# List products in float16, three one-hot matrices kept in SBUF, and an earlier gate for one layer's weights, in a sparse graph network on one core

## The chip, the cores and the metric

The kernel runs on one NeuronCore of a Trainium2 chip. The metric is the device time of one execution in microseconds, measured over several runs. One further execution was taken with the hardware profiler; its instructions, waits and DMA transfers are what the views below show. The engines are named as in the profile: PE (TensorE, with PEld for its weight loads), DVE (VectorE), ACT (ScalarE), POOL (GpSimd) and SP (SyncE, which here only issues DMAs). PSUM is the memory that PE writes its results to, SBUF the working memory, and DRAM stands for the memory outside the core.

## The reference

The input is `x`, 8 graphs of 2048 nodes with 128 features each, and one adjacency matrix `adj` (2048 x 2048, symmetric, with the diagonal set) that all layers and all eight graphs share. About 1 in 128 of its entries is set, so a node has some 17 neighbours. Four layers follow each other. Layers 0 and 2 are attention layers, cut to what matters:

```python
Q = (h @ Wq).reshape(B, N, 8, 16); K = ...; V = ...
scores = einsum('bnhd,bmhd->bhnm', Q, K) / sqrt(16)
scores = where(adj == 0, -inf, scores)
attn_out = einsum('bhnm,bmhd->bnhd', softmax(scores), V)
x = layer_norm(h + attn_out @ Wo + bo)
x = layer_norm(x + relu(x @ W1 + b1) @ W2 + b2)
```

Layers 1 and 3 are graph attention layers:

```python
h = x @ W; e = leaky_relu((h @ a_src)[:, :, None] + (h @ a_dst)[:, None, :])
e = where(adj == 0, -inf, e)
x = layer_norm(softmax(e) @ h + x)
```

Since most of the adjacency matrix is zero, only the set entries have to be computed.

## The kernel before, in words

**Gathering.** The kernel doesn't multiply by the full matrix. For each layer it writes a table in DRAM with one row per node, which holds the keys and values of all eight graphs (layers 0 and 2) or the projected features and a score (layers 1 and 3). A *unit* is 64 nodes; there are 32 units, and a *block* is two units (128 rows of `adj`). Each unit has a list of its edges, packed into nine tiles of 128 places, and the tiles are handled in four pairs and one single (`TG` is 5). For each tile POOL issues an indirect DMA (`gather`, L1647) that brings 128 table rows into SBUF: in an attention layer these are 8 KB rows, so a tile is 1 MB. A pair of tiles fills one of six `kv` buffers.

**The lists.** `block_list` and `unit_list` make them from `adj`, during the first part of layer 0 only. One adjacency block is read (L1045), DVE marks the columns (L1053) and finds up to 40 neighbours per row with repeated maximum searches (L1071 to L1096). Then PE multiplies the row degrees with constant 0/1 matrices (`before`, `upto`, `middle`, `same_unit`, `same_group`): this gives the prefix sums that say where each row's edges begin and end in the list (`places`, L1120; into the PSUM tile `ps_off`). ACT copies them beside the neighbours into the tile `aux` (`ends`, L1125). For each of the block's two units PE selects its 64 rows (`ps_aux`, L1175), ACT splits the result (`split`, L1185 to L1196), three ACT steps over 640 elements make a one-hot matrix from places to rows (`targets`, L1205 to L1209), and PE multiplies it with the neighbours (`ps_l`, L1229 to L1240). DVE picks each place's neighbour from that (`sources` and `ones`, L1255 to L1267), and ACT writes the indices for the gathers (L1277 to L1279). All these products are float32, each of which the profile records as two passes. The first four units (`LATE` is 4) have some extra steps, so that their first gathers don't need the last table rows.

**One-hot matrices.** The one-hot matrix of a unit, `hot`, is needed again by the attention layers: it spreads the unit's queries over its edges (`qe`, L1710) and adds the weighted values back per node (`acc` and `sums`, L1780). So ACT narrows it to fp8 (`hot8`, L1283), a DMA stores it to DRAM (`hots`, L1287; on POOL's queue for the first twelve units, on SP's after that), and `fetch` loads it again for each attention layer (L1362) and widens it on ACT (L1369). There are three buffers of `hot` and two of `hot8`; a `hot8` buffer is free again when its store has landed.

**Attention for a pair of tiles.** DVE multiplies the gathered keys with the spread queries (L1722) and sums over each head (L1729), ACT takes the exponential (L1739), POOL or DVE weighs the values (L1748), and PE adds them up (L1780). After the five steps of a unit come the output projection, two normalisations and the feed-forward network. The graph layers are built alike, with smaller rows.

**The setup.** Before the first gather, the table of layer 0 has to be there: the 32 units' features are loaded (L1324), projected on PE (`ps_p`, L1509), copied by ACT or DVE into one of three row buffers (`trows`, L1447 and L1449) and stored by SP (L1566). The first lists are made at the same time.

**What sets the order.** A planner (`Plan`) holds every operation with a key, estimated costs and its dependencies, simulates the engines with these costs, and so fixes the order in which each engine gets its instructions. Lower keys go first; list work of block `i` has keys about `10*i - 60`, attention work of unit `u` has keys about `5*u`, so the lists lead by about twelve units. On the chip, each engine takes its instructions strictly in that order, and waits where an input isn't ready. A buffer is taken when an operation is planned, from a fixed number per kind (`SBUF_BUFS`, `PSUM_BUFS`); `m`, the PSUM kind that lists and projections share, has two.

**Weights.** `fill` issues the small loads of a layer's weights on SP. Each load reads a *gate*, a cell whose writers must be done first. In `run`, the gate of layer 1's weights is `gates[24]`, the projection of unit 24; the later layers' gate is `x_at[8]`, the store of unit 8 of the layer before. `gat_weights` (L985) then needs PE and DVE for a few short steps (L1001 to L1018).

Of the kernel before, what the change touches and what calls it, by code (L numbers as in the profile page):

```python
# [9 lines left out]
F32 = mybir.dt.float32  # L10
# [33 lines left out]
PAIRS = TG - 1  # L44
QB = 4
# [5 lines left out]
    "kv": 6, "hot": 3, "hot8": 2, "x": 4, "q_sb": 2, "rows": 3, "at": 1, "r": 2, "x1": 2, "hidden": 1, "normed": 2,  # L51
    "xnew": 2, "trows": 2, "s": 2, "var": 2, "rstd": 2, "rc": 2, "te": 2, "e": 4, "w": 3,
    "cand": 2, "aux": 3, "unit_aux": 2, "some": 2, "rank_e": 2, "pick": 1,
# [714 lines left out]
class Sparse:  # L768
# [15 lines left out]
    def __init__(self, ctx, tc, x, xt, xk, adj, w, out):  # L784
# [42 lines left out]
        self.hots_at = [Cell() for _ in range(self.NU)]  # L827
        self.ends_at = [None] * self.NU
# [9 lines left out]
        self.shift = self.const.tile([P, LATE, 2], F32, name="shift")  # L838
# [5 lines left out]
        self.junk = self.const.tile([P, P], F32, name="junk")  # L844
# [8 lines left out]
    def constants(self):  # L853
# [49 lines left out]
        for g in range(P // GROUP):  # L903
            nc.gpsimd.memset(self.strip[g * GROUP : (g + 1) * GROUP, g, :], 1.0)
        self.before = const.tile([P, P], F32, name="before")
        nc.gpsimd.affine_select(
            out=self.before,
# [7 lines left out]
        for g in range(1, P // GROUP):  # L915
            nc.gpsimd.memset(self.before[0 : g * GROUP, g * GROUP : (g + 1) * GROUP], 0.0)
        self.upto = const.tile([P, P], F32, name="upto")
        nc.vector.tensor_tensor(self.upto, self.before, self.ident, ALU.add)
        self.same_unit = const.tile([P, P], F32, name="same_unit")
        nc.gpsimd.memset(self.same_unit, 0.0)  # L920
        for p in range(2):
            nc.gpsimd.memset(self.same_unit[p * UNIT : (p + 1) * UNIT, p * UNIT : (p + 1) * UNIT], 1.0)
        self.same_group = const.tile([P, P], F32, name="same_group")
        nc.gpsimd.memset(self.same_group, 0.0)
        for g in range(P // GROUP):
            part = slice(g * GROUP, (g + 1) * GROUP)
            nc.gpsimd.memset(self.same_group[part, part], 1.0)
        self.middle = const.tile([P, P], F32, name="middle")
        nc.vector.tensor_tensor(self.middle, self.before, self.upto, ALU.add)

        nc.vector.tensor_scalar(self.before, self.before, -1.0, None, ALU.mult)

        self.to_unit = []
        for p in range(2):
            t = const.tile([P, 2, UNIT], F32, name=f"to_unit_{p}")
            for hf in range(2):
                nc.vector.tensor_copy(t[:, hf, :], self.ident[:, p * UNIT : (p + 1) * UNIT])
            self.to_unit.append(t.rearrange("p h t -> p (h t)"))
# [99 lines left out]
    def block_list(self, adj, i):  # L1038
# [40 lines left out]
        aux = cell("aux", [P, wide])  # L1079
        some = cell("some", [P, DEG])  # L1080

        def largest(e):
            c = cand.tile.rearrange("p q c -> p (q c)")
            if late:
                e.tensor_scalar(
                    some.tile[:, 0:8], cand.tile[:, 15, :], 0.0, 0.0, ALU.is_gt, ALU.add, accum_out=aux.tile[:, WIDE + 2 : wide]
                )
            for r in range(DEG // 8):
# [5 lines left out]
                some.tile, aux.tile[:, 0:DEG], 0.0, 0.0, ALU.is_gt, ALU.add, accum_out=aux.tile[:, DEG + 4 : WIDE]  # L1094
            )
            e.tensor_reduce(self.seen[:, 1, i : i + 1], aux.tile[:, 0:DEG], axis=mybir.AxisListType.X, op=ALU.add)  # L1096
            if late:
                deg = aux.tile[:, DEG + 4 : WIDE]
                e.tensor_tensor(deg, deg, aux.tile[:, WIDE + 2 : wide], ALU.subtract)

        op({"DVE": 3.5}, largest, key + 0.2, reads=[cand], writes=[aux, some])
        ps = cell("m", [P, CH], name="ps_off")

        def places(e):
            deg = aux.tile[:, DEG + 4 : WIDE]
            after = aux.tile[:, wide - 1 : wide]
            for c, (w, x) in enumerate(
                (
                    (self.before, deg),
                    (self.upto, self.ones[:, 0:1]),  # L1110
                    (self.upto, self.ones[:, 0:1]),
                    (self.middle, deg),
                    *(
                        ((self.same_group, deg), (self.before, after), (self.middle, after), (self.upto, after))
                        if late
                        else ((self.upto, deg), (self.same_unit, deg))
                    ),
                )
            ):
                e.matmul(ps.tile[:, c : c + 1], lhsT=w, rhs=x, start=True, stop=True)  # L1120

        op({"PE": 0.8}, places, key, reads=[aux], writes=[ps])

        def ends(e):
            e.copy(aux.tile[:, DEG : DEG + 4], ps.tile[:, 0:4])  # L1125
            if not late:
                e.copy(self.seen[:, 2:4, i], ps.tile[:, 4:6])

        op({"ACT": 0.45}, ends, key + 0.3, reads=[ps], writes=[aux])
        if late:  # L1130
            self.late_places(i, aux, ps, key)
        for p in range(2):
            self.unit_list(2 * i + p, p, aux, key + 5 * p)

    def late_places(self, i, aux, ps, key):

        op = self.op
        gap = self.cell("gap", [P, 3])

        def places(e):  # L1140
            deg, after = aux.tile[:, DEG + 4 : WIDE], aux.tile[:, WIDE + 2 : WIDE + 3]
            begin, more, both = gap.tile[:, 0:1], gap.tile[:, 1:2], gap.tile[:, 2:3]
            e.tensor_scalar(begin, ps.tile[:, 4:5], float(PAIRS * P), None, ALU.max)
            e.scalar_tensor_tensor(more, ps.tile[:, 5:6], deg, begin, ALU.add, ALU.subtract)
            e.tensor_tensor(aux.tile[:, WIDE : WIDE + 1], more, ps.tile[:, 0:1], ALU.subtract)
            e.scalar_tensor_tensor(aux.tile[:, WIDE + 1 : WIDE + 2], begin, 2.0, ps.tile[:, 6:7], ALU.mult, ALU.add)
            e.tensor_tensor(self.seen[:, 2, i : i + 1], begin, ps.tile[:, 7:8], ALU.add)
            e.scalar_tensor_tensor(both, begin, 1.0 / GROUP, after, ALU.mult, ALU.add)

        op({"DVE": 0.6}, places, key + 0.3, reads=[ps], writes=[aux, gap])  # L1150
        total = self.cell("m", [P, CH], name="ps_total")
        op(
            {"PE": 0.2},
# [10 lines left out]
    def unit_list(self, u, p, block_aux, key):  # L1164
        op, cell = self.op, self.cell
        ps = cell("m", [P, CH], name="ps_aux")
        aux = cell("unit_aux", [P, 2, DEG + 3])
# [32 lines left out]


        def targets(e, f):
            oht = hot.tile[:, 0:GS]
# [11 lines left out]
        if late:  # L1215
            op({"ACT": 0.3}, lambda e: self.late_targets(e, after.tile, u), key + 0.3, reads=[ends], writes=[after])

            def both(e):
                e.tensor_scalar(after.tile, after.tile, self.late_ends[:, u, 1:2], None, ALU.is_le)
                shared = hot.tile[:, GS - P : GS]  # L1220
                e.tensor_tensor(shared, shared, after.tile, ALU.add)
# [5 lines left out]
        def parts(e):  # L1227
            for t in range(TG):
                e.matmul(  # L1229
                    ps_l.tile[:, 2 * t : 2 * t + 2, :].rearrange("p j c -> p (j c)"),  # L1230
                    lhsT=hot.tile[:, t * P : (t + 1) * P],
# [4 lines left out]
            if late:  # L1236
                e.matmul(
                    ps_l.tile[:, 2 * PAIRS : 2 * TG, DEG], lhsT=after.tile, rhs=self.shift[:, u, :], start=False, stop=False
# [3 lines left out]
                lhsT=hot.tile[:, GS - P : GS],  # L1242
# [5 lines left out]
        op({"PE": 1.0}, parts, key, reads=[hot, aux, *([after] if late else [])], writes=[ps_l])  # L1248
# [13 lines left out]
        def ones(e):  # L1262
            self.slots(e, hot, ps_l.tile[:, :, DEG + 1].rearrange("p (t j) -> p t j", j=2))
# [19 lines left out]
        op({"ACT": 1.05}, lambda e: e.activation(hot8.tile, hot.tile, AF.Copy, saturate=False), key, reads=[hot], writes=[hot8])  # L1283
# [10 lines left out]
    def slots(self, e, hot, owner):  # L1294
# [3 lines left out]
            hot.tile[:, GS:HOT].rearrange("p (t j c) -> p t j c", j=2, t=TG),  # L1298
# [906 lines left out]
```

## Time and profile before

| | |
|---|---|
| median of 3 runs | 2985.49 us (2976.74 to 2986.78) |
| the profiled execution | 2981.53 us, span 2979.8 us |
| PE, DVE, POOL, ACT busy | 79%, 77%, 72%, 47% of the span |
| first gather issued | 124.72 us |
| first multiply of attention (L1722) | 163.30 us |
| layer 0 ends, about | 1150 us |

The span runs from the first to the last instruction of the core; the profiled execution is about 1.7 us longer than its span. In the views, a line starts with the source line and the engine, then comes the operation with its output and inputs by name, and then busy time, count or mean. A wait is written as `[us <-who]`: so long was the engine idle, and that instruction or DMA ended the wait. In the table by stage, each row is a stretch of the span with the busy microseconds of each engine in it.

### The profile page before, as it was taken

To read this page: it belongs to the slowest core of one execution; us is meant where nothing else is said; L and a number is where in the kernel's file an instruction comes from. 1 tells how busy PE (TensorE), PEld (TensorE's weight loads), DVE (VectorE), ACT (ScalarE), POOL (GpSimd) and SP (SyncE) were. 2 spreads that over 40 slices of the span, in tenths; PEclk is the share of its full clock that TensorE was granted. 3 is DMA by queue.
4 is the path that set the end of the run, shared out by engine and by line. 5 is a ranking of instruction groups with operands and counts; after the bars stand their busy time and mean duration, and the time that the engine had idled before them with its cause. 6 is when DMAs were issued, how large, how long until landed. Compare 5 with 4: busy or idle time off the path is not lost. (4 is left out here: it accounts for less than half of the span.)

```text
span 2979.8 us, 60236 instructions
## 1 busy us (share of the span) xinstructions
PE 2346.3 (79%) x22064; PEld 1401.5 (47%) x22064; DVE 2302.5 (77%) x3775; ACT 1414.5 (47%) x4821; POOL 2138.6 (72%) x1459
## 2 busy tenths in 40 slices
PE   7877888888878787687777688888888887777775
PEld 6733444444433334576665243334333333566664
DVE  6779998899887777555554888988898898576665
ACT  4535555455544443455554144444444444354443
POOL 1158887788887875666664778878888786677774
PEclk8759999899999888889998789999999999887887
DMA  7749998888898886999998998999998997899996
GB/s 288 304 180 361 353 348 308 337 321 341 338 352 320 321 306 254 358 408 407 396 404 323 352 350 341 376 347 363 365 369 345 358 365 279 324 406 399 400 398 265
DMA packets 248495, 1022.93 MB, mean 343 GB/s; under 512 B 39232, under 2 KB 53312, under 8 KB 176288
## 3 DMA queue, kind: packets, MB, share of 16 engines
q0 software_dynamic: 166464, 864.44, 74.9%
q1 hardware_dynamic: 81728, 154.55, 14.1%
q8 instruction: 177, 2.90, 0.4%
q14 instruction: 126, 1.03, 0.1%
HBM read 978.59 MB, written 88.08 MB: 358 GB/s over the span
## 5 line engine op out<-in xcount | busy, mean ns | idle before, releaser
L1647 POOL DMA_INDIRECT kv<-table,idx x1152 | 1198.0, 1040 | 588.0 <-issue 285.2
L1748 POOL TENSOR_TENSOR kv<-kv 128x2048 f32<-128x2048 f32 (+1 forms) x259 | 926.6, 3589 | 96.9 <-ACT kv L1739 92.7
L1722 DVE TENSOR_TENSOR kv<-qe,kv 128x2048 f32<-128x2048 f32 (+1 forms) x320 | 662.0, 2069 | 115.0 <-DMA kv<-table,idx 69.9
L1729 DVE TENSOR_REDUCE s<-kv 128x128 f32<-128x2048 f32 (+1 forms) x320 | 659.5, 2061 | 9.3
L1710 PE MATMUL qe<-q_sb,hot 32*128 32x512 f32 (+1 forms) x2304 | 398.2, 695 | 156.0 <-DVE kv L1722 152.3
L1780 PE MATMUL acc<-kv,hot 128*32 128x512 f32 (+1 forms) x2304 | 370.0, 656 | 47.0 <-POOL kv L1748 24.7
L1984 PE MATMUL acc_q<-kv,w 128*32 128x129 f32 (+1 forms) x4608 | 202.1, 308 | 121.5 <-DVE w L1968 96.9
L1968 DVE TENSOR_TENSOR w<-hot,e 128x512 f32<-128x512 f32 (+1 forms) x384 | 221.2, 597 | 50.3 <-ACT e L1958 37.0
L1710 PEld LDWEIGHTS qe<-q_sb,hot 32*128 32x128 f32 (+1 forms) x2304 | 106.7, 196 | 289.5 <-DVE kv L1722 235.2
L1739 ACT ACTIVATE kv<-s 128x128 f32<-128x128 f32 (+1 forms) x320 | 95.3, 298 | 300.2 <-DVE s L1729 193.2
L1984 PEld LDWEIGHTS acc_q<-kv,w 128*32 128x32 f32 (+1 forms) x4608 | 158.2, 126 | 151.5 <-DVE w L1968 109.5
L1946 DVE TENSOR_TENSOR e<-te,kv 128x16 f32<-128x16 f32 (+1 forms) x320 | 58.3, 182 | 215.7 <-DMA kv<-table,idx 212.8
L1583 ACT ACTIVATE junk<-ps_c 128x128 f32<-128x128 f32 x494 | 136.5, 276 | 158.6 <-PE ps_c L1471 140.7
L1447 ACT COPY trows<-ps_p 128x258 f32<-128x258 f32 (+1 forms) x240 | 113.8, 476 | 187.9 <-PE ps_p L1511 103.7
L1780 PEld LDWEIGHTS sums<-kv,hot 128*32 128x32 f32 (+1 forms) x2304 | 90.1, 120 | 212.4 <-issue 206.8
L1958 ACT ACTIVATE e<-e 128x16 f32<-128x16 f32 (+1 forms) x320 | 64.9, 212 | 243.6 <-DVE e L1953 238.3
L1471 PE MATMUL ps_c<-centre,r 128*128 128x128 f32 x1024 | 153.3, 296 | 32.3 <-DVE r L1857 15.6
L1481 PE MATMUL ps_f<-x,W 128*128 128x512 f32 (+1 forms) x264 | 155.7, 674 | 23.5 <-ACT hidden L1877 16.2
L1471 PEld LDWEIGHTS ps_c<-centre,r 128*128 128x128 f32 x1024 | 132.3, 202 | 74.1 <-DVE r L1857 33.7
L1984 PE MATMUL acc<-kv,w 128*32 128x129 f32 (+1 forms) x2304 | 116.4, 303 | 50.1 <-DVE w L1968 36.2
L1887 PE MATMUL ps_y<-hidden,W 128*128 128x512 f32 (+1 forms) x264 | 146.7, 644 | 6.2 <-ACT hidden L1877 5.7
L1780 PEld LDWEIGHTS acc<-kv,hot 128*32 128x32 f32 (+1 forms) x2304 | 55.7, 115 | 197.6 <-issue 107.6
(201 smaller groups left out, 4015.2 us busy)
## 6 DMA issues: line engine op xcount, KB each, us to landing
x<-xd SPq DMA_DIRECT2D x96, 256.0 KB
xd<-xnew SPq DMA_DIRECT2D x93, 256.0 KB
kv<-table,idx POOLq DMA_INDIRECT x1152
table<-trows SPq DMA_DIRECT2D x128, 130.0 KB
kv<-adj_dram SPq DMA_DIRECT2D x16, 1024.0 KB
table<-trows SPq DMA_DIRECT2D x32, 512.0 KB
table<-trows SPq DMA_DIRECT2D x64, 256.0 KB
kv<-xk_dram SPq DMA_DIRECT2D x8, 1024.0 KB
```

Of the source, the lines that this page charges most:

```text
L1471: e.matmul(ps.tile[:, cols], lhsT=flat(x.tile)[:, cols], rhs=self.centre, start=True, stop=True)
L1481: lambda e: e.matmul(ps.tile, lhsT=w, rhs=x.tile, start=True, stop=True),
L1583: e.activation(self.junk, x, AF.Square, scale=P**-0.5, accum_out=var.tile[:, b, 1:2])
L1647: e.indirect_dma_start(out=rows(kv.tile, j), out_offset=None, in_=self.tables[n][0:nodes], in_offset=bass.IndirectOffsetOnAxis(ap=self.idx ...
L1710: e.matmul(qe.tile[:, j, hf, :], lhsT=hot.tile[rows, t * P : (t + 1) * P], rhs=q.tile[rows, :], start=True, stop=True,)
L1722: e.tensor_tensor(k, qe.tile[:, 0:tiles].rearrange("p j h c -> p (j h) c"), k, ALU.mult)
L1729: e.tensor_reduce(s.tile[:, 0 : tiles * heads].rearrange("p (q c) -> p q c", q=2 * tiles), k, axis=mybir.AxisListType.X, op=ALU.add,)
L1748: e.tensor_tensor(v, v, w.unsqueeze(3).to_broadcast([P, 2 * tiles, heads // 2, HD]), ALU.mult)
L1780: e.matmul(out[rows, :], lhsT=hot.tile[:, col : col + GROUP * (3 - tiles)], rhs=rhs[:, 2 * j + hf, :], start=(t == 0), stop=(t == TG - 1),)
L1887: lambda e, f=f, ps=ps: e.matmul(ps.tile, lhsT=L["W2"][:, f, :], rhs=hidden.tile[:, f, :], start=(f == 0), stop=(f == FFN // P - 1),),
L1968: e.tensor_tensor(w.tile[:, :, j : j + tiles, :].rearrange("p x j c -> p j x c"), oh[:, j : j + tiles].unsqueeze(2).to_broadcast(shape), e ...
L1984: e.matmul(acc(b)[at : at + GROUP * (3 - tiles), :], lhsT=w.tile[:, hf * hb + b, j : j + 3 - tiles, :].rearrange("p j c -> p (j c)"), rhs= ...
```

## The change

It has three parts.

**Float16 lists.** The constant matrices `before`, `same_unit`, `same_group` and `to_unit`, the tiles `unit_aux`, `gap` and `shift`, and a new tile `aux16` are float16, and the one-hot matrix of a list is written as float16 into half of the same `hot` buffer; `upto` and `middle` are gone. Per block there are two products in `places` (three for the first two blocks) in place of six (eight). The ends of the rows, which were products of their own, are now computed on ACT from the row's begin and its degree; the place of a row in its group is a constant, `number`. A new ACT operation, `narrow`, copies the neighbours and degrees from `aux` to `aux16`. Some constants are set by DVE instead of POOL. All values are small whole numbers, which float16 holds.

**Kept matrices.** `hot8` has five buffers. `unit_list` remembers each unit's `hot8`, and for the first three units of layer 0 `fetch` copies from that tile, with no load; their stores to DRAM remain, since layer 2 reads them.

**Gate.** Layer 1's weights have the gate `x_at[3]` instead of `gates[24]`.

```diff
+KEPT = 3
-    "kv": 6, "hot": 3, "hot8": 2, "x": 4, ...
+    "kv": 6, "hot": 3, "hot8": 5, "x": 4, ...
...
+        aux16 = cell("aux16", [P, wide], F16)
+        def narrow(e):
+            e.copy(aux16.tile[:, 0:DEG], aux.tile[:, 0:DEG])
+            e.copy(aux16.tile[:, DEG + 4 : WIDE], aux.tile[:, DEG : DEG + 1])
+            if late:
+                e.copy(aux16.tile[:, WIDE + 2 : wide], aux.tile[:, DEG + 1 :])
+            e.copy(aux16.tile[:, DEG + 1 : DEG + 3], self.number)
+        op({"ACT": 0.7}, narrow, key + 0.2, reads=[aux], writes=[aux16])
         def places(e):
-            deg = aux.tile[:, DEG + 4 : WIDE]
-            after = aux.tile[:, wide - 1 : wide]
-            for c, (w, x) in enumerate(
-                (
-                    (self.before, deg),
-                    (self.upto, self.ones[:, 0:1]),
-                    (self.upto, self.ones[:, 0:1]),
-                    (self.middle, deg),
-                    *(
-                        ((self.same_group, deg), (self.before, after), (self.middle, after), (self.upto, after))
-                        if late
-                        else ((self.upto, deg), (self.same_unit, deg))
-                    ),
-                )
-            ):
-                e.matmul(ps.tile[:, c : c + 1], lhsT=w, rhs=x, start=True, stop=True)
-        op({"PE": 0.8}, places, key, reads=[aux], writes=[ps])
+            deg = aux16.tile[:, DEG + 4 : WIDE]
+            e.matmul(ps.tile[:, 0:1], lhsT=self.before, rhs=deg, start=True, stop=True)
+            if late:
+                e.matmul(ps.tile[:, 1:2], lhsT=self.same_group, rhs=deg, start=True, stop=True)
+                e.matmul(ps.tile[:, 2:3], lhsT=self.before, rhs=aux16.tile[:, WIDE + 2 : wide], start=True, stop=True)
+            else:
+                e.matmul(ps.tile[:, 1:2], lhsT=self.same_unit, rhs=deg, start=True, stop=True)
+        op({"PE": 0.4}, places, key, reads=[aux16], writes=[ps])
         def ends(e):
-            e.copy(aux.tile[:, DEG : DEG + 4], ps.tile[:, 0:4])
+            e.copy(aux16.tile[:, DEG : DEG + 1], ps.tile[:, 0:1])
+            deg = aux.tile[:, DEG : DEG + 1]
+            e.activation(aux16.tile[:, DEG + 3 : DEG + 4], ps.tile[:, 0:1], AF.Identity, bias=deg, scale=-2.0)
             if not late:
-                e.copy(self.seen[:, 2:4, i], ps.tile[:, 4:6])
+                e.activation(self.seen[:, 2, i : i + 1], ps.tile[:, 0:1], AF.Identity, bias=deg, scale=-1.0)
+                e.copy(self.seen[:, 3, i : i + 1], ps.tile[:, 1:2])
...
-        aux = cell("unit_aux", [P, 2, DEG + 3])
+        aux = cell("unit_aux", [P, 2, DEG + 3], F16)
...
+        def hot16():
+            return hot.tile[:, 0 : HOT // 2].bitcast(F16)
...
-        op({"PE": 1.0}, parts, key, reads=[hot, aux, *([after] if late else [])], writes=[ps_l])
+        op({"PE": 0.8}, parts, key, reads=[hot, aux, *([after] if late else [])], writes=[ps_l])
...
         hot8 = cell("hot8", [P, HOT], F8)
+        self.kept[u] = hot8
...
         hot = self.cell("hot", [P, HOT])
+        if n == 0 and u < KEPT:
+            hot8 = self.kept[u]
+            self.op({"ACT": 1.05}, lambda e: e.copy(hot.tile, hot8.tile), key - 15, reads=[hot8], writes=[hot])
+            return x, hot
         if LAYERS[n] is MHA:
...
         self.gate = self.gates[16]
         self.layers[0] = self.mha_weights(0)
-        self.gate = self.gates[24]
+        self.gate = self.x_at[3]
         for n, kind in enumerate(LAYERS):
```

## The prediction

> **What bounds the kernel now.** I read the page first, then the busy time by stage, then the waits of SP and the timeline of the stage that the change touches. Page, head and part 1:
>
> ```profile
> span 2979.8 us, 60236 instructions
> PE 2346.3 (79%) x22064; PEld 1401.5 (47%) x22064; DVE 2302.5 (77%) x3775; ACT 1414.5 (47%) x4821; POOL 2138.6 (72%) x1459
> ```
>
> No engine is full over the span, so stages decide. Busy time by stage (columns: us, then PE, PEld, DVE, ACT, POOL, then PE clock, DMA share, GB/s); cuts at the first gather, the first multiply of attention, the start of unit 4, the end of the lists and the end of layer 0:
>
> ```profile
> 0.00:124.70 124.70, 97.69 (x432) 79.56 (x432) 88.06 (x328) 64.61 (x165) 10.47 (x42) 0.85 0.76 281
> 124.70:163.30 38.60, 29.93 (x125) 26.35 (x125) 15.73 (x50) 19.75 (x61) 13.43 (x15) 0.51 0.83 330
> 163.30:285.20 121.90, 94.66 (x595) 44.37 (x596) 109.88 (x129) 48.79 (x141) 93.26 (x50) 0.76 0.69 260
> 285.20:700.00 414.80, 342.93 (x2359) 175.54 (x2358) 384.53 (x514) 222.60 (x724) 329.92 (x178) 0.92 0.88 332
> 700.00:1150.00 450.00, 360.91 (x2486) 174.69 (x2484) 370.93 (x291) 205.27 (x692) 356.62 (x194) 0.93 0.85 323
> ```
>
> From 163.3 to 700 DVE is 92% busy (494.4 of 536.7): it carries attention and the rest of the lists, and is the bound. Before 163.3 it is busy 103.8 and idle 59.5. Up to 124.7 PE leads (97.7); from there to 163.3 nobody leads: 38.6 us pass with DVE busy 15.7. Every microsecond of DVE idleness removed before 163.3 moves the DVE-bound stretch, and all behind it, forward. What is waited for there, from SP's waits and the timelines of the engines:
>
> ```profile
> SPq L1362 <- DMA hots<-hot: 45.9, 3, 24.4
> 152.31 8.72 SPq L1362 DMA_DIRECT2D hot<-hots  x2
> 124.72 1.07 POOL L1647 DMA_INDIRECT kv<-table,idx  x1 [7.51 <-PE ps_p L1509]
> 136.36 0.56 POOL L1287 DMA_DIRECT2D hots<-hot  x1 [0.86 <-ACT ends L1186]
> 139.07 0.60 ACT L1805 COPY q_sb<-ps_q 128x512 f32<-128x512 f32 x1
> 160.08 1.01 ACT L1369 CAST hot<-hot 128x960 f32<-128x960 fp8e5 x1
> 161.14 2.09 PE L1710 MATMUL qe<-q_sb,hot 32*128 32x512 f32 x8 [1.66 <-ACT hot L1369]
> 163.30 2.29 DVE L1722 TENSOR_TENSOR kv<-qe,kv 128x2048 f32<-128x2048 f32 x1 [2.17 <-PE qe L1710]
> ```
>
> The queries are in SBUF at 139.7, but SP fetches the first one-hot matrix only at 152.3: it needs one of two `hot8` buffers, and their stores, issued on POOL's queue at 134.9 and 136.4 behind eight 1 MB gathers, land 16 us later. The spread (161.1) and the multiply (163.3) follow. In the PE groups of the setup (7 to 125 us) the list products are these and their like:
>
> ```profile
> L1509 PE MATMUL ps_p<-Wkv,kv 128*128 128x256 f32 x252 | 77.1, 462 | 21.0 <-ACT trows L1447 8.0 <-DMA kv<-xk_dram 7.4 <-ACT seen L1127 2.7
> L1229 PE MATMUL ps_l<-unit_aux,hot 128*128 128x86 f32 x60 | 7.8, 280 | 0.0
> L1120 PE MATMUL ps_off<-ones,upto 128*128 128x1 f32 x24 | 4.0, 269 | 0.0
> ```
>
> All list groups of that view sum to 30.8 us (ps_off 15.8, ps_l with its two corrections 11.2, ps_aux 3.1, ps_total 0.7); each float32 product stands as two passes of about 0.28 us.
>
> [...]
>
> **The change, part by part.**
>
> *Kept matrices.* Units 0 to 2 lose SP's load and its wait; the copy reads the kept fp8 tile. In the changed program's order on ACT, unit 0's copy stands among the last projections, long before the query copy, so the spread then waits for `q_sb` alone. With the setup as it is: last row copy ends at 127.3 (DVE, L1449). Between it and the query copy ACT has 7.4 us: one index set with its fp8 copy (0.30+0.25+0.16+1.01), two `unit_aux`/`ends` sets (0.94 each), the three 640-wide steps (0.82+0.85+0.75), four small copies (0.75), the query copy (0.60). I allow 5 for hand-overs (ACT waited 4.9 and 5.7 there in two places). Then four small ACT steps 0.75, which free a PSUM buffer, ps_aux 0.3, the spread 2.1, hops 1: first multiply at 144. The first pair of gathers, 2 MB at 400 GB/s from 124.7, is in by about 132: not late. So 163.3 becomes 144: -19.3.
>
> *Half-width and fewer products.* Up to the last projection the new order has 12 ps_off, 9 ps_aux, 2 ps_total and 52 ps_l products (eight units, not six). [...] Bounds: nothing, if a 16-bit product costs two passes; 19, if PE alone set the pace. DVE (88 of 124.7) and ACT come next, and two more units' list work (ACT some 11 us) now falls into the setup, so I take half: -9.
>
> *ACT and DVE around it.* Each block gains narrowing copies and a scaled step, about 0.75 us of ACT net; 16 blocks make 12 us on an engine 54% busy while the lists run, covered by DVE's backlog and a list lead of twelve units; the five blocks before the first multiply would cost 3.8 if exposed. Memsets move from POOL to DVE ahead of the first adjacency row, where DVE stood idle: nothing. The other DVE instructions keep their sizes.
>
> *Weights of layer 1.* The new gate is `x_at[3]`, but at that point of `run` no store of unit 3 exists, so the gate is empty. In the order the five loads stand as SP's 9th to 13th DMAs, before the first table store. This frees 3.1 us of SP at 109 to 113, where stores wait for ACT's rows anyway: nothing. At the start each of SP's DMAs waits for an earlier one eight places back, so the first three stores (13.5 to 16.5 before) now wait for the second and third adjacency loads (15.4 and at most 23.5), and ACT for row buffers behind them (it waited 5.7 and 0.9 there): bounds 0 and +6; I take +2. ps_w and the six DVE steps (1.3 us) move early too, same work; their 8.1 us stall at 155 goes with them and is inside the -19.3.
>
> *Sum.* First multiply at 163.3 - 19.3 - 9 + 2 = 137. The new order has done nine units' picks by then, not eleven: 2 x 2.33 = 4.7 us of DVE comes back. By unit 4 both orders hold the same DVE work (15 picks, 10 adjacency passes, 9 searches), so idle time is what counts: 59.5 before, 137 - 99.1 = 37.9 after: -21.6. From 163 to 700 DVE also waits 4.3 for ps_l and 10.3 for the spread; shorter list products ahead of them on PE give about 4. From the end of layer 0 on, the order of every engine is identical, so the shift is carried: -26. On the profiled execution 2981.53 (span 2979.8) that is 2955.5; on the median 2985.49, which lies 4 above it, 2959.
>
> **Rivals.** *Setup shrinks by all of PE's 19* (PE leads with 97.7; against it: DVE then needs 93 of some 105): 10 more, 2949 or below. *Setup doesn't shrink* (late first stores, the extra ACT step, PSUM's two `m` buffers): the round trip alone, -19.3 + 4.7 - 4, and +2 to +6 for the stores: about 2970. *The stall is refilled by another:* the kept matrices hold two of three `hot` buffers while lists are made, or gathers, DMA share 0.88 from 285 on, become the bound. Then the gain shrinks to under 9: 2981. Against it: the share is 0.69 until 285, and four units (38 MB) fit into the 140 us from a gather at 118 to unit 4 at 259. *Slower:* POOL is in order, and the eighth one-hot store now stands after only two gathers, waiting for ACT's fp8 copy, seven gathers behind it, and one more store ahead of the first weighing. Before, such stores held POOL 8.3 and 8.0 us. If the copy waits for the whole list chain, gathers starve; it takes 35 us (26 + 9) of starvation to pass 0.3% on the slow side, so about 2996. Against it: the chain is done within some 10 us of the last projection. That the weights don't load behind unit 4 I hold as certain; it is in the sum.
>
> **How the numbers follow.** 0.3%, 9 us, is about what a measurement of this kernel can tell from no change. Main case 0.56 (own range 2950 to 2967); setup fully shorter 0.12; round trip alone 0.18; refilled 0.08; slower 0.06. The first three are faster by over 9: 0.86. Range: 2939 (setup at its bound plus shorter PE waits all along) to 2977 (round trip alone, with late stores).
>
> **What would show it.** Right: SP no longer waits on `hots` before the first spread; the first multiply stands near 137, its releaser the spread behind `q_sb`; ps_l passes number 5 a unit at under 0.2; unit 4 starts near 260; layers 1 to 3 keep their lengths. Wrong: a first gather later than 124.7, a wait on `trows` or `hots` in the first 40 us that is longer than before, DVE waiting on gathers before unit 4, or a layer that changes length after 1150.

## The result and the profile after

The changed kernel takes 2961.92 us in the median (2960.0 to 2966.09) where the kernel before, timed beside it, takes 2985.65: a ratio of 0.993, interval 0.9911 to 0.995. Its profiled execution took 2960.0 us, with a span of 2958.3. The forecast was 2959 (2955.5 for the profiled execution), so the total was met within 3 us on the median. What lies under it was met only in part. The page's head and first part, changed kernel:

```profile
span 2958.3 us, 59482 instructions
PE 2282.4 (77%) x21668; PEld 1334.4 (45%) x21668; DVE 2305.8 (78%) x3785; ACT 1423.9 (48%) x4899; POOL 2137.4 (72%) x1455
```

PE lost 64 us of work (2346.3 to 2282.4), the other engines none: the gain is in idle time. Busy time by stage, with the columns as before and the cuts at this kernel's own first gather, first multiply and unit 4:

```profile
0.00:129.10 129.10, 84.21 (x337) 61.95 (x337) 97.78 (x371) 74.08 (x209) 10.29 (x39) 0.80 0.75 276
129.10:139.95 10.85, 6.24 (x35) 4.42 (x35) 2.08 (x5) 8.49 (x33) 8.69 (x9) 0.69 0.92 329
139.95:264.10 124.15, 83.42 (x563) 34.74 (x567) 113.49 (x133) 52.77 (x155) 98.48 (x55) 0.78 0.86 332
```

The first row was to shrink from 124.7 to about 118 and grew to 129.1. The second was to go from 38.6 to some 19 and went to 10.9: most of DVE's list work of that gap (15.73 us before, 2.08 now) lies ahead of the first gather (DVE 97.78 there, before 88.06). Together the first multiply moved from 163.30 to 139.95, where 137 was forecast. The timelines of POOL, ACT and DVE, with the wait of each instruction in brackets:

```profile
129.13 1.07 POOL L1671 DMA_INDIRECT kv<-table,idx  x1 [6.33 <-PE ps_off L1129]
107.65 0.99 ACT L1380 CAST hot<-hot 128x960 f32<-128x960 fp8e5 x1
132.71 0.59 ACT L1829 COPY q_sb<-ps_q 128x512 f32<-128x512 f32 x1 [0.40 <-PE ps_off L1129]
131.52 0.61 POOL L1307 DMA_DIRECT2D hots<-hot  x1
139.95 2.29 DVE L1746 TENSOR_TENSOR kv<-qe,kv 128x2048 f32<-128x2048 f32 x1 [3.93 <-DMA kv<-table,idx]
```

Unit 0's copy (L1380) runs 25 us ahead of the queries, as read from the order, and `q_sb` sets the spread. But the multiply then waits for its gather, which the forecast had called not late: with a first gather at 129 instead of 118 it is. (The first pair of tiles lands 10.8 us after its issue, where the forecast had allowed some 7. Its 400 GB/s were about what all transfers together reach while the setup loads, 365 to 440 GB/s from 4 to 28 us of the kernel before; from 129.1 to 139.95 here they reach 329.) Two of the prediction's own signs of being wrong thus came: a first gather later than 124.7, and DVE waiting for gathers before unit 4, 10.9 us in all where it was 0.6 before. The one-hot store between the gathers (L1307) waited for nothing, so the rival on POOL's order did not happen. Unit 4 starts at 264.09, before 285.25: -21.2, where -21.6 was forecast. The span is 21.5 us shorter.

The list products in the PE groups of the setup (7 to 125 us):

```profile
L1533 PE MATMUL ps_p<-Wkv,kv 128*128 128x256 f32 x252 | 78.8, 469 | 24.7 <-ACT seen L1139 8.5 <-DMA kv<-xk_dram 7.6 <-ACT trows L1471 4.1
L1248 PE MATMUL ps_l<-unit_aux,hot 128*128 128x86 f16 x40 | 3.4, 229 | 3.4 <-ACT hot L1228 2.7 <-ACT trows L1471 0.7
L1124 PE MATMUL ps_off<-aux,before 128*128 128x1 f16 x5 | 0.8, 164 | 3.8 <-ACT ends L1200 1.4 <-ACT owner L1298 1.4 <-ACT trows L1471 0.7
L1009 PE MATMUL ps_w<-ident,Wx 128*128 128x128 f32 x1 | 0.4, 448 | 6.5 <-DMA Wx<-L_W_dram 6.5
```

A float16 product is one pass, as forecast (160 of `ps_l` at L1248 in layer 0, before 320 at L1229), of 0.16 to 0.23 us in the mean; a float32 one was two of 0.23 to 0.30 us. All list groups of this view sum to 9.2 us instead of 30.8. PE waits more in return: 24.7 us ahead of the projections (before 21.0) and 6.5 for layer 1's early weights.

In the table below are the starts of some units of layer 0 (the first multiply of each), for every profile. Two studies ran on chips where the kernel before takes 3201 and 3206 us, the last on one where it takes 2976; so each ratio is against the kernel before on the same chip. Layer 0 hardly differs between chips (rows 1 and 2, 3 and 4), but one profile is one execution: the two repeats differ from their first profiles by up to 7 us at a unit's start, and the runs of one kernel spread by 10 us and more to each side. Late positions are good to about 10 us.

| kernel | first gather | unit 0 | unit 4 | unit 10 | unit 22 | unit 31 | ratio (interval) |
|---|---|---|---|---|---|---|---|
| before | 124.7 | 163.3 | 285.3 | 469.9 | 839.2 | 1112.7 | 1 |
| before, again | 125.5 | 164.2 | 288.6 | 477.2 | 843.6 | 1120.0 | 1.0012 (0.9997 to 1.0027) |
| changed | 129.1 | 140.0 | 264.1 | 462.6 | 818.8 | 1095.4 | 0.993 (0.9911 to 0.995) |
| changed, again | 127.7 | 139.0 | 264.0 | 462.7 | 819.6 | 1091.9 | 0.9921 (0.9898 to 0.9945) |
| kept matrices alone | 122.0 | 140.9 | 280.1 | 482.0 | 865.2 | 1138.3 | 1.0072 (1.0047 to 1.0097) |
| float16 alone | 121.1 | 155.9 | 278.8 | 480.3 | 843.6 | 1111.6 | 0.9936 (0.9898 to 0.9975) |
| early gate alone | 129.9 | 172.2 | 291.3 | 484.5 | 858.3 | 1127.3 | 1.0007 (0.9991 to 1.0023) |
| changed, old gate | 121.2 | 131.9 | 270.5 | 455.3 | 843.1 | 1111.7 | 0.9936 (0.9907 to 0.9966) |
| changed, delayed | 127.5 | 161.2 | 283.6 | 481.3 | 843.0 | 1119.1 | 0.9979 (0.9963 to 0.9995) |
| changed, products four times | 127.7 | 138.9 | 266.1 | 464.8 | 826.4 | 1108.0 | 0.9949 (0.993 to 0.9968) |
| kept, order of before | 124.9 | 163.0 | 281.1 | 466.1 | 832.1 | 1102.0 | 1.0002 (0.9987 to 1.0018) |
| float16, order of before | 118.9 | 155.5 | 273.3 | 458.9 | 823.4 | 1096.3 | 0.9948 (0.993 to 0.9965) |
| both, order of before | 119.0 | 154.4 | 272.4 | 457.1 | 819.6 | 1087.6 | 0.9939 (0.9918 to 0.996) |
| changed, loads moved back | 127.9 | 137.9 | 267.9 | 466.4 | 820.0 | 1093.5 | 0.9921 (0.9897 to 0.9946) |

### The profile page after: what moved, and what is told of

Same layout as the page of the kernel before. It is cut to its first block, busy times and chain, and to the rows that moved or that the text cites. A ratio compares the mean times of both kernels' runs of the same rounds, so it can differ in the third digit from the quotient of the medians.

```text
span 2958.3 us, 59482 instructions
## 1 busy us (share of the span) xinstructions
PE 2282.4 (77%) x21668; PEld 1334.4 (45%) x21668; DVE 2305.8 (78%) x3785; ACT 1423.9 (48%) x4899; POOL 2137.4 (72%) x1455
## 5 line engine op out<-in xcount | busy, mean ns | idle before, releaser
L1471 ACT COPY trows<-ps_p 128x512 f32<-128x512 f32 (+1 forms) x238 | 112.8, 475 | 178.2 <-PE ps_p L1535 100.0
L1640 ACT ACTIVATE normed<-ps_c,rstd 128x128 f32<-128x128 f32 x495 | 143.2, 370 | 5.7 <-DVE normed L1642 3.8
```

The costliest lines, as they stand in the source:

```text
L1640: e.activation(out, in_, AF.Copy, scale=by)
```

## The experiments

### One part at a time

Four kernels, each planned anew: the kernel before with the kept matrices and five `hot8` buffers; the changed kernel with neither of these and the old gate, which leaves the float16 lists; the kernel before with the new gate; and the changed kernel with the old gate. The letters of the theories are those of each study.

```diff
kept matrices alone (on the kernel before)
+KEPT = 3
+    "hot8": 5,
+        if n == 0 and u < KEPT: (copy from self.kept[u], as in the change)
float16 alone (on the changed kernel)
-KEPT = 3
+KEPT = 0
-    "hot8": 5,
+    "hot8": 2,
-        self.gate = self.x_at[3]
+        self.gate = self.gates[24]
early gate alone (on the kernel before)
-        self.gate = self.gates[24]
+        self.gate = self.x_at[3]
changed, old gate (on the changed kernel)
-        self.gate = self.x_at[3]
+        self.gate = self.gates[24]
```

Expected of the kept matrices alone:

> The kernel before with the second part of the change alone: five buffers of hot8, and the first three units' one-hot matrices copied from SBUF. Theory A (the round trip of the one-hot matrices through DRAM is where the time came from): first gather near 125 as before, first multiply near 144 instead of 163, time 15 to 20 us below before. Theory B (the shorter list products on PE are where it came from): the first multiply moves little, 0 to 4 us below before.

Expected of the float16 lists alone:

> The kernel before with the float16 lists alone: two hot8 buffers, every one-hot matrix through DRAM, the old gate. Theory A: SP still waits for the stores of the one-hot matrices, the first multiply stays at 158 to 165, time 0 to 4 us below before. Theory B: PE's list time in the setup falls from 31 to some 10 us, the first gather comes at 110 to 118, and the time is 15 to 20 us below before. Theory C (the three parts only work together, since the setup is a chain of in-order hand-overs): the setup gets longer, and the time is above before.

Expected of the early gate alone:

> The kernel before with the new gate alone. Theory A: the five loads stand before the first table store, the first gather comes 2 to 5 us later than 124.7, and the time is within 5 us of before, on either side. Theory D (taking the weights and their DVE steps out of the stretch from 109 to 157 is worth as much as the round trip): 10 us or more below before.

Expected of the changed kernel with the old gate:

> The changed kernel with the old gate, so that the layer 1 weights load behind the projection of unit 24 again. If the early loads cost the setup its 4.4 us (first gather at 129.1 instead of 124.7): first gather at 122 to 126, time 3 to 6 us below the changed kernel, some 2957. If the new gate is worth what it takes: first gather the same or later, time at 2962 or above.

At the first multiply the parts add up: against 164.2 the kept matrices bring 23.2 us, float16 8.3, and the early gate takes 8.0; the sum, -23.5, stands beside -25.2 for all three. At the end they don't. The kept matrices alone start attention 23 us earlier and end 0.7% later; float16 alone has 0.64% although its start is 24 us behind that of the changed kernel with the old gate, which has the same 0.64%. So for the kept matrices theory A was right at the first multiply and wrong at the end. For the float16 lists theory B's time came nearly (14 us below by the medians, 20 by the ratio), but not its first gather (121.1 instead of 110 to 118).

The kept kernel loses its head start early: at unit 4 it is 8.5 us ahead of the repeat of the kernel before, at unit 10 4.8 us behind. Between units 14 and 22 (617.1 and 865.2, before 613.2 and 843.6) it loses another 18 us. Timelines of POOL and DVE in that later stretch, kept matrices alone:

```profile
796.71 3.68 POOL L1755 TENSOR_TENSOR kv<-kv 128x2048 f32<-128x2048 f32 x1 [17.00 <-ACT kv L1746]
785.68 0.17 DVE L1556 TENSOR_TENSOR t<-ps_p,strip 128x8 f32<-128x8 f32 x1 [7.65 <-PE ps_p L1518]
```

POOL stands for 17 us ahead of a weighing, with the next gathers behind it. Busy time by stage there, kept matrices alone and then the kernel before on a chip of the same speed:

```profile
760.00:850.00 90.00, 72.89 (x506) 39.49 (x498) 66.28 (x61) 48.32 (x157) 63.80 (x35) 0.92 0.78 291
```

```profile
760.00:850.00 90.00, 74.47 (x530) 36.27 (x529) 78.64 (x66) 45.12 (x142) 75.91 (x44) 0.94 0.94 364
```

No kept matrix is in use there any more. These lines show where the time goes, not why. Either a head start is used up in the middle of layer 0 whatever is done (if POOL, ACT and DVE set the pace there together), or the planner, which makes a new order for each of these kernels, had made a bad one. The next study tells these apart.

### The start delayed, and the products issued four times

The changed kernel was run again, and in two variants that the planner doesn't see, so that each engine has the very same order. One has ten useless reductions on DVE ahead of the first multiply; the other issues the list products four times over.

```diff
changed, delayed (in multiply)
+                if late:    # layer 0, unit 0, first pair
+                    for _ in range(10):
+                        e.tensor_reduce(self.waste..., k..., axis=X, op=ALU.add)
                 e.tensor_tensor(k, qe.tile[:, 0:tiles]..., k, ALU.mult)
changed, products four times (in parts; the same in places and for ps_aux)
+            for again in (False, False, False, True):
                 for t in range(TG):
                     e.matmul(ps_l.tile[:, 2 * t : 2 * t + 2, :]..., start=True,
-                             stop=t < TG - 1)
+                             stop=not again or t < TG - 1)
```

Expected of the kernel before, again:

> The kernel before once more, unchanged, for a profile on the same chip as the three other runs and as a measure of what its timing can tell from no change. Every theory: ratio 1.000 within 0.003, and unit starts that give the base for the others.

Expected of the changed kernel, again:

> The changed kernel once more, for the same chip and for how well the start of a unit repeats. Every theory: ratio between 0.991 and 0.996; the start of unit 22 within 5 us of that in a repeat on a chip of the same speed.

Expected of the delayed kernel:

> The changed kernel with ten reductions of 2.3 us each put on DVE ahead of the first multiply of unit 0 (23 us of useless work whose result nobody reads; the planner doesn't see it, so that the order of every engine is the same but for these ten). Theory A, that of the prediction (from the first multiply on DVE sets the pace, and each microsecond of start is carried): the end comes 20 to 23 us later than the changed kernel's, ratio to it 1.007, ratio to the kernel before about 1.000. Theory B (the gathers and the in-order loop between POOL, ACT and DVE set the pace after unit 4, and a head start at unit 0 is used up there, as the first four runs look): the first multiply comes about 23 us later, unit 22 and the end at most 6 us later, ratio to the kernel before 0.991 to 0.996.

Expected with the products four times:

> The changed kernel with each float16 product of the lists (ps_off, ps_aux and the five ps_l of a unit) issued four times over, with the same result; the order on all other engines is the same. PE's list time in layer 0 goes from about 31 us back to about 103, where the kernel before has 116. Theory C (the PE time of the list products, between the spreads and the sums of attention, is what the change gains in layer 0): slower than the changed kernel by 12 to 25 us, ratio to the kernel before 0.997 to 1.002, with the loss growing evenly from unit 4 to unit 22. Theory A (only idle time of DVE ahead of the first multiply counts): at most 8 us slower, all of it ahead of the first multiply.

The repeats agree with the first profiles in layer 0: unit 22 within 1 us for the changed kernel, within 5 for the kernel before. DVE's timeline in the delayed kernel:

```profile
137.94 23.17 DVE L1749 TENSOR_REDUCE waste<-kv 128x128 f32<-128x2048 f32 x10 [3.09 <-DMA kv<-table,idx]
161.21 2.29 DVE L1755 TENSOR_TENSOR kv<-qe,kv 128x2048 f32<-128x2048 f32 x1
```

The first multiply comes at 161.2 instead of 139.0, 22.2 us later, and the median goes from 3179.45 to 3199.41, 20.0 us later. Theory A holds: **with the order unchanged, the head start reaches the end: 20.0 of 22.2 us**. (The intervals of the two ratios leave some 9 us to each side of these 20, so it is anything from half of it to all; the 6 us of theory B lie outside, and unit 22 comes 23 us later too.) In this order a head start is not lost in the middle of layer 0.

The repeated products were to bring PE's list time in layer 0 from 31 us to about 103. They brought it to 59.7, since repeated products overlap (52 ns of PE's busy time each, against 77 for those issued once); the largest group, first of the changed kernel again, then with the products four times:

```profile
L1248 PE MATMUL ps_l<-unit_aux,hot 128*128 128x86 f16 x160 | 12.3, 214 | 9.9 <-ACT hot L1228 2.9 <-ACT x L1650 2.2 <-ACT trows L1471 1.7
```

```profile
L1253 PE MATMUL ps_l<-unit_aux,hot 128*128 128x86 f16 x640 | 33.4, 216 | 10.2 <-DVE t L1578 2.6 <-ACT hot L1232 2.5 <-ACT x L1655 2.2
```

So 29 us of PE time were put back, of the 85 that the change takes out of layer 0 (115.3 to 30.5, all list groups). This cost 11.5 us at the end (3190.96 against 3179.45; the two intervals overlap, and the difference is uncertain by some 10 us), about the least that theory C asked for. The loss grows from 2 us at unit 10 to 7 at unit 22 and 16 at unit 31. Just as telling is the setup. There the list groups went from 9.2 to 17.8 us, and the first gather stayed at 127.7, the first multiply at 138.9. In the changed kernel's order, PE's list time in the setup is hidden.

### The order held

Here the parts were put into the order of the kernel before. The planner sees the old operations with the old costs; only what is issued differs. For the kept matrices the three loads are planned and not issued, and the kept tiles have three buffers of their own, with the two of `hot8` left to all else as before. For float16 the narrowing copies are issued right ahead of the products that read them. The fourth kernel keeps the changed kernel's order and only moves the five loads of layer 1's weights back behind the projection of unit 24, and the steps on PE and DVE that use them to about 10 us ahead of the first gather.

```diff
kept, order of before (in fetch; both loads and copies stay planned)
+            held = n == 0 and u < KEPT
-            hot8 = self.cell("hot8", [P, HOT], F8)
+            hot8 = Cell("hot8", lambda: self.kept[u].tile) if held else self.cell("hot8", [P, HOT], F8)
-                lambda e: e.dma_start(out=hot8.tile, in_=self.hots[u]),
+                lambda e: held or e.dma_start(out=hot8.tile, in_=self.hots[u]),
float16, order of before (on the changed kernel, KEPT = 0, old gate and buffers)
         def places(e):
+            aux16.tile = (a float16 buffer)
+            narrow(self.nc.scalar)
-        op({"ACT": 0.7}, narrow, key + 0.2, reads=[aux], writes=[aux16])
-        op({"PE": 0.4}, places, key, reads=[aux16], writes=[ps])
+        op({"PE": 0.8}, places, key, reads=[aux], writes=[ps])
changed, loads moved back (in issue)
+        order = [o for o in order if id(o) not in late]
+        order[at:at] = loads                        # behind gates[24]
+        order[free[0] + 1 : free[0] + 1] = steps    # where no PSUM buffer is held
```

Expected of the kept matrices in the order of before:

> The kernel before with the three kept matrices, planned as if the three loads were still there: the order of every engine is that of the kernel before, only SP's three loads are gone. The first study of the kept matrices let the planner make a new order, and ended 0.7% slower although the first multiply came 23 us earlier. Theory O (a head start is carried wherever the order stays the same; what the new order does between units 4 and 22 comes on top, in either direction): first multiply 141 to 146, units 10 and 22 at least 14 us earlier than before, ratio 0.9935 to 0.9955. Theory K (kept matrices lose their head start in the middle of layer 0 whatever the order, since something other than DVE sets the pace there): first multiply the same, unit 22 within 6 us of the kernel before or later, ratio 0.998 to 1.007.

Expected of float16 in the order of before:

> The kernel before with the float16 lists alone, planned with the old costs; the narrowing copies stand on ACT right ahead of the products that read them, and the order of all else is that of the kernel before. Theory O: first multiply 6 to 10 us earlier, then the 85 us less of PE time in layer 0 give 8 to 12 us more between units 0 and 22 (issuing each product four times cost 11.5 us at the end), unit 22 14 to 22 us earlier, ratio 0.993 to 0.996. Theory P (the gain of the float16 lists came from the planner's new order): first multiply the same, unit 22 and the end at most 10 us earlier, ratio 0.997 to 1.000.

Expected of both:

> Both parts together in the order of the kernel before, and layer 1's weights where they were. Theory O: the sum of the two runs above, first multiply at 132 to 138, unit 22 28 to 40 us earlier than before, ratio 0.987 to 0.991, which would be below the changed kernel. Theory K: as the float16 lists alone, ratio 0.993 to 0.995.

Expected with the loads moved back:

> The changed kernel in its own order, but with the loads of layer 1's weights put back behind the projection of unit 24 and their seven short steps shortly ahead of the first multiply; nothing else moves. Theory O: without the early loads the first gather comes at 121 to 123 instead of 127.7, the first multiply at 131 to 134 instead of 139, units 10 and 22 5 to 8 us earlier than in the changed kernel, ratio to the kernel before 0.9895 to 0.991 (the changed kernel has 0.992). If the early loads cost nothing at the end (the gathers of the first units catch up), the ratio stays at 0.992.

*Kept matrices.* Both theories missed at the first multiply, which stays at 163.0; the ratio is 1.0002. The timelines of ACT and POOL show why. With the loads gone, ACT stops all the same, for the stores:

```profile
144.58 0.99 POOL L1654 DMA_INDIRECT kv<-table,idx  x1 [0.99 <-DMA kv<-table,idx]
152.19 1.00 ACT L1289 ACTIVATE hot<-hot 128x960 fp8e5<-128x960 f32 x1 [5.62 <-DMA hots<-hot]
153.82 0.56 ACT L1812 COPY q_sb<-ps_q 128x512 f32<-128x512 f32 x1
153.49 0.62 POOL L1293 DMA_DIRECT2D hots<-hot  x1 [7.92 <-ACT hot L1289]
159.75 1.01 ACT L1376 CAST hot<-kept 128x960 f32<-128x960 fp8e5 x1
```

The step that narrows a later unit's matrix to fp8 (L1289) needs a free `hot8` buffer, and both wait for their stores behind the gathers. Unit 0's copy (L1376) has its data since long, but stands behind that step in ACT's order. The kernel before had stood at the same step at the same time. Its timelines, ACT's and one line of PE's:

```profile
152.52 1.00 ACT L1283 ACTIVATE hot<-hot 128x960 fp8e5<-128x960 f32 x1 [4.23 <-DMA hots<-hot]
154.76 0.47 PE L1001 MATMUL ps_w<-ident,Wx 128*128 128x128 f32 x1 [2.59 <-ACT q_sb L1805]
159.51 0.48 ACT L1185 ACTIVATE unit_aux<-ps_aux,strip 128x43 f32<-128x43 f32 x2 [3.30 <-PE ps_aux L1175]
160.08 1.01 ACT L1369 CAST hot<-hot 128x960 f32<-128x960 fp8e5 x1
```

The copy (L1369) has no wait in brackets: its load had come in time. What held it was ACT's narrowing step (L1283, which starts at 152.5). PE's step on layer 1's weights (L1001) was released by the ACT copy of `q_sb` behind that step, and ACT then waited for the `ps_aux` that PE made after it. With the loads gone the same chain ends within 0.4 us of where it did. So the load of the one-hot matrix was not the wait to remove; the wait was for the buffers. The change escapes it with five buffers, the copy's early place, or both: from 100 to 165 us the changed kernel's ACT doesn't wait for `hots` at all. Which of the two suffices was not tried.

*Float16.* In the old order the first gather comes at 118.9 (-5.8), the first multiply at 155.5 (-7.8), unit 22 at 823.4 (-15.8), and the ratio is 0.9948. Theory O's figures hold: the gain of the float16 lists is not the planner's doing. *Both* together have 0.9939, not the 0.987 to 0.991 of theory O, since the kept matrices add nothing that can be measured in that order. Taken together: in no pair of runs do the kept matrices bring a measurable gain at the end (alone 1.0072 in an order of their own and 1.0002 in the old one; beside the float16 lists 0.9936 with and without them where the planner made the order, 0.9939 against 0.9948 in the old order). These pairs could have missed 8 us in the old order and 16 in the planner's, and the changed kernel's own order was not tried with the loads put back; what the kept matrices are worth there stays open. The float16 lists alone bring 14 to 20 us, in the old order as in one of their own.

*Loads.* Putting the loads back changes nothing: first gather 127.9, ratio 0.9921. SP's timeline with the loads moved back, then POOL's:

```profile
102.69 0.92 SPq L975 DMA_DIRECT2D Wx<-L_W_dram  x1
```

```profile
127.88 1.07 POOL L1692 DMA_INDIRECT kv<-table,idx  x1 [8.20 <-PE ps_p L1554]
```

So the 4 to 7 us by which the first gather comes later with the new gate (129.9 against 125.5; 127.7 against 121.2) are not the price of the early transfers, nor of PE's 6.5 us of waiting for them. What remains is the order that the planner makes when these operations come early. In it more list work stands ahead of the first gather; with the old gate, DVE is 89.1 us and ACT 70.7 us busy there, instead of 97.8 and 74.1:

```profile
0.00:121.22 121.22, 84.26 (x328) 62.48 (x328) 89.11 (x339) 70.68 (x194) 9.77 (x39) 0.82 0.78 290
```

That this work is what delays the gather is likely, but not shown. The same comparison bears on the question of the first study: with the loads late and the changed kernel's order, unit 22 starts at 820.0; with the loads late and a new order (changed, old gate) at 843.1, though it was 6 us ahead at unit 0. Allowing 10 us for the one execution, some of this is the order. At the end only 5 us of it are left (0.9936 against 0.9921, with intervals that overlap), so its size stays open.

No kernel tried is clearly below the changed one; moving the loads back gives the same ratio.

## Why the prediction was right, and where not

The total (-23.7 on the median, forecast -26) is right, and so is the assumption that idle time of DVE ahead of the first multiply counts and is carried to the end, in the one order in which this was tested. But that the sum came out is in part luck. The term that it took for the largest, the kept matrices (-19.3, some -15 after the list work that comes back), is found at the end in no pair of runs that tried it. The float16 lists, with -9 and -4 in the sum, bring 14 to 20 of the 24 to 27 us by themselves, and what a new order gives or takes had no term. Point by point:

- **What bounds the kernel.** "Every microsecond of DVE idleness removed before 163.3 moves the DVE-bound stretch": in the changed kernel's order the delay shows 20.0 of 22.2 us. Unit 4 came at -21.2 (forecast -21.6), and the end of the span at -21.5. From one order to another it does not hold: the kept matrices alone start attention 23 us earlier and end later.
- **Kept matrices, -19.3.** The gap from the first gather to the first multiply lost 27.8 us (38.6 to 10.9), so the term was too small. Its reason was half right. That the copy moves ahead on ACT was read from the order, and this is what happened. That "units 0 to 2 lose SP's load and its wait" is worth nothing by itself: with the order held and the loads gone, the first multiply stays at 163.0. The prediction had quoted the two `hot8` buffers, but put the wait on the load, although the line that it showed for the copy (160.08) has no wait; the wait stood on ACT's narrowing step before it. (Of the two waits of ACT "there" behind its 5 us for hand-overs, the 4.9 stand in that stretch, at 131; a wait of 5.75 comes only at 187.5.)
- **Half-width and fewer products, -9 in the setup.** This is the step that failed. The first gather came 4.4 us later instead of 7 earlier (-9 +2). The PE time of the lists shrank by 21.6 us (30.8 to 9.2), where the step had 19 up to a slightly later point, its author's estimate of what shorter passes save, which no trace showed at that time. But in the new order that time is hidden: twice of it moved nothing (17.8 us, first gather 127.7 in both). The error has two parts. With the old gate the changed kernel's first gather comes at 121.2, 3.5 us earlier than before instead of 9. With the new gate it comes 6.5 to 7.9 later than that, where the next step had put +2. What the setup then has more is list work that the step had named and set against half of PE's gain (by the first gather DVE is busy 97.8 us, before 88.1, and ACT 74.1, before 64.6); that it sets the later gather is argued, not shown. In the old order the step would have been nearer: 5.8 us at the first gather, 7.8 at the first multiply. The errors at the two places, -8.5 in the gap and +11.4 in the setup, nearly cancelled, in part because list work moved from the one to the other.
- **Early weights, +2.** The loads do stand where the order showed them, and the first table stores do go out later (15.5, with the loads moved back 12.5). They wait as the step had it: 2.1, 2.3 and 2.1 us for the loads of adjacency, features and adjacency that SP issued eight DMAs before each; in the kernel before, SP's 36th to 38th DMAs wait in the same way for the 28th to 30th, 2.5 us at most. But moving the five loads back gives nothing at the first gather (0.2 us). With a planner, the price of a moved load can lie in the order that it causes and not in its transfer; alone, the early gate costs 8 us at the first multiply and nothing that can be measured at the end.
- **Shorter products ahead of attention, -4.** Too small. From reading two of DVE's waits the prediction gave 4 us to the stretch from 163 to 700. Putting back a third of the PE time saved costs 11.5 us, most of it after unit 10, and with float16 in the old order unit 22 gains 8 us more than the first multiply did. A likely reason, not shown, is that the list products stand in PE's order between DVE's reads and the next spread, so that their time counts also where they aren't named as the last releaser. The 20 us for the start and 11.5 for a third of the PE time add up to more than the 27 that the change brought in that study. With some 10 us of uncertainty on each the excess is not clear; if it is real, the two overlap or the new order costs something in the middle. This stays open.
- **The rivals.** The refilled stall, "2981", is what the kept matrices alone did, and worse: slower by 0.7%. A third of what they lose up to unit 22 (15 of 45 us) goes by unit 4, while kept matrices are in use; the rest goes where none is, so there the cause that the rival named first, `hot` buffers held, isn't it. Its other cause, gathers as the bound, isn't seen from 760 to 850 us either, with a DMA share of 0.78 against 0.94. What the cause is stays open. The rival in which the setup doesn't shrink had its premise right and its time (2970) wrong, since the gap behind the setup shrank by more than either took. In the slower rival POOL's stores were to stall between the gathers; they did not.
- **Weight loads.** The weight load of a `ps_off` product with `before` takes 104 ns in the mean in float16 (L1124, 16 of them) and 220 ns in float32 (L1120, 36 passes), that of a `ps_l` product 106 ns (L1248, 160) and 224 ns (L1229, 320).

## What to carry to other kernels

Where a planner fixes the order, change one thing with the order held before giving it a cause: here a part that looked worth 23 us at its own place was worth nothing measurable at the end where it was tried, and a load that looked dear was free. Before a wait is put down to a step, look whether that step's own line has one: the copy here had none, and the wait to remove stood several lines earlier on the same engine. When a load waits for a buffer, ask who else in the same in-order queue takes buffers of that kind, since taking the load away can leave the next one waiting for a store, as it left ACT's narrowing step here (5.62 us). A delay that the planner doesn't see, put where the head start is won, is the cheapest test of whether the head start reaches the end.

## What the runs showed that was not expected

Four repeats of a 128x86 float16 product with 128 weights cost 33.4 us of PE's busy time for 640, 52 ns each, against 77 ns each for 160 unrepeated ones, though the mean length of one is the same (216 and 214 ns): back to back they overlap. And on chips where the whole kernel is 7 to 8% slower (before 3206.29 us against 2985.65, changed 3179.45 against 2961.92), layer 0 takes the same time to within 1% (unit 31 starts at 1120.0 against 1112.7, and at 1091.9 against 1095.4). What takes longer behind it isn't shown.
